# Attention on one core: the first query tile of each group without transposes on TensorE

## The chip, the cores and the metric

The kernel runs on one core of a Trainium2 chip. A core has a matrix engine (TensorE, PE in the profile, with its weight loads as PEld), a vector engine (VectorE, DVE), a scalar engine (ScalarE, ACT), a general one (GpSimd, POOL) and a queue that issues transfers (SyncE, SP). They run side by side and wait for each other by semaphores. PE's results land in PSUM, eight banks of 128 x 512 float32; DVE and ACT carry them from there to SBUF. The metric is the time on the device in microseconds, as the median of several runs.

## The reference

For x of 4 x 512 tokens with 256 features: a layer norm, then attention and a feed-forward gate on the normed tokens, and x + attention * gate at the end. There are 16 query heads of 128 and 4 key heads; query head h uses key head h mod 4, so a key head serves a group of four.

```python
xn = layernorm(x)
Q, K, V = xn @ Wq + bq, xn @ Wk + bk, xn @ Wv + bv     # 16, 4 and 4 heads of 128
scores = Q K^T / sqrt(128) + causal mask               # 512 x 512 of each head
ctx = softmax(scores) @ V
y = gelu(ctx @ Wo + bo)
s = layernorm(xn + y) * gamma + beta
g = silu((silu(xn @ Wgate) * (xn @ Wup)) @ Wdown)
out = x + s * g
```

All is float32, and the mask is causal: a query sees the keys up to its own place.

## The kernel before

A float32 product is made of three PE products. Each operand is split into `hi`, a rounded part, and `lo`, the rest; `product` (line 93) adds hi*hi, hi*lo and lo*hi into one PSUM bank (lines 95, 96 and 97). Splitting a bank is the work of `split_psum` (line 82): ACT writes `hi` (line 86, or 89 with a bias), then DVE writes `lo` (line 87, or 90).

The feed-forward gates of all four batches come first, up to about 150 us. The attention phase follows: 64 steps (b, g, i), for each batch b, group g and query tile i of 128 queries, i from 0 to 3 (in the very last group from 3 to 0). A query tile holds four sub-tiles of 32 queries (S = 32); one tile of scores has 128 rows, 32 queries of each of the four heads.

- `scores` (line 416) takes one sub-tile: PE makes the scores (for i = 0 with whole float32 operands, line 438), DVE adds the mask and takes the row's least (line 449), ACT takes exp and the row's sum (line 460), DVE inverts the sum (line 473), and POOL scales the row (line 474). The probabilities lie in `p`, rows of heads and queries, columns of keys. Two constant buffers of 128 x 4 x 512 serve in turn; a first query tile uses the last 128 of the 512 columns.
- `transposed_probs` (line 476) turns the 128 keys of block j so that keys are rows: four transposes on PE against the identity (line 481) into a bank "t", then a split into a pair of SBUF tiles `pT`, from a tag "pt" of four buffers.
- `weighted` (line 486) multiplies the turned probabilities with the values of block j: one `product` with 128 rows (keys), 128 weight columns (features) and 512 moving columns (four heads of 128 queries). The sum over j lies in the bank "c"; the last block's split adds the values' bias and gives `ctxT`.
- `projected` (line 505) multiplies `ctxT` with Wo, in steps of one head, into "y0" or "y1".
- `keys`, `values` and `queries` (lines 375, 386 and 401) make the operands of later steps; each puts its product in the bank "mm" once attention runs.

PSUM's eight banks are two "s" (scores), two "t", "mm", "c", "y0" and "y1".

The order around the change is written by hand. In the loop over the steps (line 632) each piece of work gets a position, a number from a table of constants, and the pieces are emitted in that order: scores of the next step, transposes and products of this one, the projection of the step before, and queries, keys or values for later ones. From the emitted order a scheduler, with its own costs, sets each engine's queue and gives buffers to tiles; within an engine's queue the order is then fixed, and a waiting instruction holds all that stand behind it. Transfers stand in SP's queue: transposed tokens and what the end of a batch wants (`reload`, `load_fin`), weights (`load_w`), and the output.

Of the kernel before, what the change touches and what calls it, by code (L numbers as in the profile page):

```python
# [17 lines left out]
P = 128  # L18
EPS = 1e-5
S = 32  # queries of a head in a tile of scores  # L20
# [6 lines left out]
def kernel(  # L27
    ctx: ExitStack,
    tc: tile.TileContext,
    x: bass.AP,  # [B, L, D]  # L30
    wq: bass.AP,  # [D, H*E]
    bqT: bass.AP,  # [E, H]
    wk: bass.AP,  # [D, KV*E]
    bkT: bass.AP,  # [E, KV]
    wv: bass.AP,  # [D, KV*E]
    bvT: bass.AP,  # [E, KV]
    wo: bass.AP,  # [H*E, D]
    bo: bass.AP,  # [D]
    gamma: bass.AP,  # [D]
    beta: bass.AP,  # [D]  # L40
    wguT: bass.AP,  # [D, 2*INTER]
    wdT: bass.AP,  # [INTER, D]
    out: bass.AP,  # [B, L, D]
):
    """Products of float32 operands run on the tensor engine as products of two
    parts each: hi, rounded to the engine's 12 significant bits, and lo, the exact
    rest. hi*hi + hi*lo + lo*hi, summed in float32, is the float32 product."""
# [6 lines left out]
    G = H // KV  # query heads of a key head: g, g + KV, ...  # L54
    INTER = wdT.shape[0]
    NT = L // P  # token tiles of a batch
    ND = D // P  # chunks of the model dimension
    NI = INTER // P  # chunks of the inner dimension
# [10 lines left out]
    @contextmanager  # L69
    def behind(*keys):  # L70
        """Queues what the block does behind these instructions on their engines."""
        with ExitStack() as stack:
            for k in keys:
                for ins in latest[k]:
                    stack.enter_context(tc.issue_after(ins.ins))
            yield

# [1 line left out]
    def pair(tag, bufs, name, n=512):  # L79
        return work.tile([P, 2, n], F32R, tag=tag, bufs=bufs, name=name)  # L80

    def split_psum(dst, src, bias=None):
        """dst[:, 0] = hi, dst[:, 1] = lo of a bank of PSUM (plus a bias per partition)."""
# [9 lines left out]
    def product(out_ap, lhs, rhs, first, last, **kw):  # L93
        """out += lhs^T rhs; lhs and rhs are (hi, lo)."""
# [4 lines left out]
    # The power -1/2 of a variance.  # L99
    mhalf = const.tile([P, NT], F32, name="mhalf")  # L100
    nc.gpsimd.memset(mhalf, -0.5)
    # Loads the scalar engine's table before it is needed.
# [11 lines left out]
    def load_w(name, views, hi_on=None, lo_on=None):  # L114
        """A slot of 1024 columns of weights, in two parts."""
# [17 lines left out]
    # Probabilities of a query tile: [32 queries of each head of a group, sub-tile of 32  # L133
    # queries, keys], the last key that the tile sees in the last column. What a sub-tile
    # doesn't see of the last P keys stays zero.
# [20 lines left out]
    # The first tokens and the first weights come in small pieces, in the order of their use.  # L156
# [14 lines left out]
    def split_first(f, lo_on=None):  # L171
        """The columns of f of the first slot of the gate's weights."""
# [8 lines left out]
    # Keeps the tensor engine busy until the first tokens are there, so that its clock is up by then.  # L181
# [22 lines left out]
    # What the attention phase wants back: the transposed tokens in two parts, and for  # L204
    # the end of a batch the normed tokens, gate * gamma and gate * beta + x.
# [13 lines left out]
    def transposed(b, t):  # L219
        """xT[b][c]: the normed tokens, transposed, of chunk c, in two parts."""  # L220
# [31 lines left out]

    # The last S keys that a tile of scores sees hold the diagonal of each head. Masked
    # before the scores are scaled.
# [41 lines left out]
    ff_tags = [("s", 2), ("s", 2), ("t", 2), ("t", 2), ("mm", 1), ("c", 1)]  # L296
    def h_tiles(b):
        """Places for the eight tiles of a batch among those of the attention phase."""
# [65 lines left out]
    banks = ["mm", "c"]  # "c" only until the first values are weighted  # L364
# [5 lines left out]
    def whole(dst, t):  # L370
        """The first P columns as they were before they were split: so few columns go
        faster through the tensor engine whole."""
        nc.gpsimd.tensor_tensor(dst, t[:, 0].bitcast(F32), t[:, 1].bitcast(F32), ALU.add)  # L373
# [12 lines left out]
    def values(b, t):  # L386
# [12 lines left out]
        vv[b, t] = v  # L399

    def queries(b, g, r):
# [6 lines left out]
        if r == 0:  # L408
            # [E, part, sub-tile of S queries, head of g, query]
# [6 lines left out]
    def scores(b, g, i, t):  # L416
        """Causal scores of sub-tile t of query tile i, of the four heads of g, as
        probabilities. Kept negated up to exp, so that the minimum of a row is the bias
        that exp wants."""
# [3 lines left out]
        if t == 0:  # L423
            if (b, g, i) in steps[-3:]:
                # Towards the end the slots of weights that are done with serve as well.
# [50 lines left out]
    def transposed_probs(b, g, i, j):  # L476
        p = probs[b, g, i][0]
        # From rows [head, query] of each sub-tile to columns [head, sub-tile, query].
# [7 lines left out]
    def weighted(b, g, i, j):  # L486
        """Transposed probabilities against the values: [E, heads of g, queries of i]."""
# [7 lines left out]
        if j == i:  # L495
            c = pair("stage" if (b, g, i) == steps[-1] else "ctx", 2, f"ctxT_{b}_{g}_{i}")
            # A row of probabilities sums to 1, so the values' bias comes in here.
# [36 lines left out]
    def finished(b, t, last):  # L534
        """Residual, second layer norm, gate and the outer residual of token tile t."""
# [213 lines left out]
```

## Time and profile before

| what | value |
|---|---|
| median of three runs | 681.08 us (680.22 to 681.22) |
| span of the profiled execution | 679.5 us |
| PE busy | 661.7 us, 97% of the span |
| PE weight loads busy | 581.6 us, 86% |
| DVE busy | 447.8 us, 66% |
| ACT busy | 402.6 us, 59% |
| POOL busy | 273.4 us, 40% |
| transposes of probabilities on PE (line 481) | 640, 273 ns each |
| products with the values on PE (lines 95 to 97, pc) | 480, 395 to 432 ns each |
| bytes moved by transfers | 34.7 MB |

One execution was profiled, and all durations come from it. Its span runs from the first to the last instruction; the runs' times are taken by themselves and are not sums of the profile's rows. In a row of the groups, the name before `<-` is written and the names after it are read: `pt` are turned probabilities in PSUM, `pT` their split in SBUF, `pc` the context's sum, `ctxT` its split, `ps` scores, `pq`, `pk` and `pv` queries, keys and values, `py` the projection. Durations of matmuls overlap, so how closely they follow one another is read from their starts. A row of stretches gives its bounds and length, then the busy time and number of instructions per engine, then the granted clock, the DMA share and GB/s. In the list of the steps' ends that the stretches follow, the mark is the end of the ACT half of a `ctxT` split.

### The profile page before, as it was taken

What the parts mean: (1) busy time and instruction counts of PE and PEld (TensorE: products, weight loads), DVE (VectorE), ACT (ScalarE), POOL (GpSimd) and SP (SyncE); (2) the same over time, 40 slices, a digit from 0 to 9 for tenths busy, and PEclk for the clock granted to TensorE, in tenths of its full rate; (3) what the DMA queues carried; (4) which work ended last, traced back from release to release, by engine and by line L of the source; (5) the groups of instructions that cost most, each with busy time, mean ns of one, the idle gap of its engine ahead of it and who ended that gap; (6) DMA issues with size and microseconds to landing.
All of it is one profiled execution on the core that took longest, in us unless ns stands there. A gap on an engine that the chain in (4) does not pass through costs nothing.

```text
span 679.5 us, 12006 instructions
## 1 busy us (share of the span) xinstructions
PE 661.7 (97%) x3996; PEld 581.6 (86%) x3996; DVE 447.8 (66%) x1337; ACT 402.6 (59%) x956; POOL 273.4 (40%) x490
## 2 busy tenths in 40 slices
PE   7979999999999999999999999999999999999995
PEld 6768888889889888888888898889888988888984
DVE  5864434165766766775787666668867766687867
ACT  4434333253765766677676665957666668576772
POOL 5588130720646423222353232216433323354332
PEclk8999999999999999999999999999999999999998
DMA  7753322211310100000022000002210000032000
GB/s 223 246 191 122 127 81 90 77 47 50 92 31 2 36 29 1 1 0 1 20 76 94 1 0 1 2 1 63 63 62 1 1 2 1 1 93 79 1 1 32
DMA packets 25262, 34.73 MB, mean 51 GB/s; under 512 B 2288, under 2 KB 18544, under 8 KB 25200
## 3 DMA queue, kind: packets, MB, share of 16 engines
q1 hardware_dynamic: 25200, 33.97, 15.4%
q8 instruction: 31, 0.51, 0.3%
q14 instruction: 31, 0.25, 0.1%
HBM read 21.38 MB, written 12.58 MB: 50 GB/s over the span
## 4 chain that ended last, share of the span: by engine, by line
PE 89%; DVE 4%; DMA 4%; issue 1%; ACT 1%; POOL 1%; SPq 0%; ACTq 0%; DVEq 0%; POOLq 0%
PE pt L481 10%; PE pc L96 5%; PE pc L95 5%; PE pc L97 5%; PE pq L95 5%; PE py L97 4%; PE ps L97 4%; PE ps L96 4%; PE pq L97 4%; PE pq L96 4%; PE py L95 4%; PE ps L95 4%; PE py L96 4%; PE pg L97 3%; PE pg L96 3%; PE pg L95 3%
## 5 line engine op out<-in xcount | busy, mean ns | idle before, releaser
L474 POOL TENSOR_SCALAR p<-p,total 128x320 f32<-128x320 f32 (+15 forms) x256 | 127.6, 505 | 195.5 <-DVE total L473 174.9
L460 ACT ACTIVATE p<-p,least 128x320 f32<-128x320 f32 (+15 forms) x256 | 133.2, 522 | 59.7 <-DVE least L449 51.0
L449 DVE CUSTOM_DVE_ANT_0 p<-ps,mask 128x320 f32<-128x320 f32 (+15 forms) x256 | 109.8, 435 | 42.6 <-PE ps L97 17.5
L86 ACT CAST pT<-pt 128x512 fp32r<-128x512 f32 x160 | 89.2, 587 | 60.0 <-PE pt L481 59.2
L87 DVE TENSOR_TENSOR pT<-pt,pT 128x512 fp32r<-128x512 f32 x160 | 106.6, 686 | 25.5 <-ACT pT L86 25.0
L481 PE MATMUL pt<-ident,p 128*128 128x128 f32 x640 | 107.2, 273 | 0.5 <-POOL p L474 0.5
L481 PEld LDWEIGHTS pt<-ident,p 128*128 128x128 f32 x640 | 81.1, 142 | 17.5 <-POOL p L474 0.7
L97 PE MATMUL py<-w_o,ctxT 128*128 128x256 f32 x256 | 73.5, 287 | 0.6 <-DVE ctxT L90 0.6
L95 PE MATMUL py<-w_o,ctxT 128*128 128x256 f32 x256 | 72.9, 285 | 0.1
L96 PE MATMUL py<-w_o,ctxT 128*128 128x256 f32 x256 | 72.1, 281 | 0.0
L96 PE MATMUL pc<-pT,v 128*128 128x512 f32 x160 | 69.1, 432 | 0.0
L95 PE MATMUL ps<-kT,qT 128*128 128x288 f32 (+3 forms) x192 | 68.5, 357 | 0.0
L373 POOL TENSOR_TENSOR q<-qT 128x128 f32<-128x128 f32 x64 | 30.4, 474 | 93.7 <-DVE qT L90 55.8
L95 PE MATMUL pc<-pT,v 128*128 128x512 f32 x160 | 64.5, 403 | 0.1
L97 PE MATMUL pc<-pT,v 128*128 128x512 f32 x160 | 63.2, 395 | 0.0
L473 DVE RECIPROCAL total<-total 128x1 f32<-128x1 f32 x256 | 38.4, 158 | 37.2 <-ACT p L460 35.1
L96 PE MATMUL ps<-kT,qT 128*128 128x288 f32 (+3 forms) x192 | 62.2, 324 | 0.0
L97 PE MATMUL ps<-kT,qT 128*128 128x288 f32 (+3 forms) x192 | 61.7, 322 | 0.0
L90 DVE SCALAR_TENSOR_TENSOR qT<-pq,bq_sb,qT 128x512 fp32r<-128x512 f32 x64 | 47.9, 748 | 15.3 <-ACT qT L89 15.3
L89 ACT ACTIVATE qT<-pq,bq_sb 128x512 fp32r<-128x512 f32 x64 | 44.0, 687 | 20.1 <-PE pq L97 19.6
L90 DVE SCALAR_TENSOR_TENSOR ctxT<-pc,bv_sb,ctxT 128x512 fp32r<-128x512 f32 x64 | 47.8, 747 | 11.1 <-ACT ctxT L89 10.5
L95 PE MATMUL pg<-xT,w_gu 128*128 128x512 f32 (+1 forms) x132 | 50.5, 397 | 3.9 <-DVE h L338 2.5
(127 smaller groups left out, 1567.5 us busy)
## 6 DMA issues: line engine op xcount, KB each, us to landing
fin<-fin_dram SPq DMA_DIRECT2D x16, 384.0 KB, 3.2
xT_dram<-xT SPq DMA_DIRECT2D x8, 512.0 KB, 2.6
fin_dram<-gate SPq DMA_DIRECT2D x16, 256.0 KB, 2.0
xT_again<-xT_dram SPq DMA_DIRECT2D x8, 512.0 KB, 3.9
fin_dram<-xn SPq DMA_DIRECT2D x16, 128.0 KB, 2.4
st_q<-in_wq_dram SPq DMA_DIRECT2D x8, 256.0 KB, 3.2
st_o<-in_wo_dram SPq DMA_DIRECT2D x4, 512.0 KB, 3.9
out_dram<-y SPq DMA_DIRECT2D x16, 128.0 KB, 1.7
```

The source lines that it names most:

```text
L86: first = nc.scalar.copy(hi, src)
L87: second = nc.vector.tensor_tensor(lo, src, hi.bitcast(F32), ALU.subtract)
L89: first = nc.scalar.activation(hi, src, AF.Identity, bias=bias)
L90: second = nc.vector.scalar_tensor_tensor(lo, src, bias, hi.bitcast(F32), ALU.add, ALU.subtract)
L95: nc.tensor.matmul(out_ap, lhs[0], rhs[0], start=first, stop=False, **kw)
L96: nc.tensor.matmul(out_ap, lhs[0], rhs[1], start=False, stop=False, **kw)
L97: nc.tensor.matmul(out_ap, lhs[1], rhs[0], start=False, stop=last, **kw)
L449: nc.vector.tensor_tensor_reduce(pr, ps[:, :seen], mask[:, L - seen :], scale=-SCALE, scalar=HIGHEST, op0=ALU.add, op1=ALU.min, accum_out= ...
L460: exp = nc.scalar.activation(pr, pr, AF.Exp, bias=least[:, r : r + 1], scale=-1.0, accum_out=total[:, r : r + 1],)
L473: latest["dve"] = [nc.vector.reciprocal(total[:, r : r + 1], total[:, r : r + 1])]
L474: latest["pool"] = [nc.gpsimd.tensor_scalar(pr, pr, total[:, r : r + 1], 1.0, ALU.mult, ALU.mult)]
L481: nc.tensor.transpose(pt[:, :, t], p[:, t, ts(j, P)], ident)
```

## The change

For a first query tile (i = 0) that is not among the last three steps, which is 15 of 16, the probabilities are no longer turned on PE. DVE transposes each sub-tile in blocks of 32 x 32: a block holds 32 queries of one head against 32 keys, so afterwards the rows are [head, 32 keys] and the columns [key block, sub-tile, query]. Blocks that the mask leaves empty are skipped. The result `u` lies in columns of the same constant buffer that this tile does not use, and ACT and DVE split it as before, now from SBUF.

The values have to meet these rows. `values` of the first token tile of a batch writes its pair to DRAM (`v_dram`), and `values_beside` reads it back for each group so that all four sets of 32 rows hold the same 128 keys as four blocks of 32 (`vr`, from the tag "pt"). `weighted` then makes, for each key block, each of the three parts and each head, a product of 32 rows whose place in the array is the head's row group. A key block c meets the queries from 32c on, so the columns are 128, 96, 64 or 32. Each head has its own PSUM bank, "c", "t", "t" and "mm", and is split by itself: four splits of 128 columns in place of one of 512.

`values_beside` is emitted for groups 1 to 3 at position 0.9 of the step with i = 2 of the group before, for group 0 of batches 1 to 3 at the start of the step that uses it, and for batch 0 ahead of the loop. Comments and docstrings are removed as well.

```diff
@@ values
         vv[b, t] = v
+        if t == 0:
+            nc.sync.dma_start(v_dram[b].rearrange("g p s e -> p s g e"), v.bitcast(F32).rearrange("p s (g e) -> p s g e", g=KV))
+
+    def values_beside(b, g):
+        vr[b, g] = work.tile([P, P // S, 2, E], F32R, tag="pt", bufs=4, name=f"vr_{b}_{g}")
+        for r in range(G):
+            nc.sync.dma_start(vr[b, g][ts(r, S)].bitcast(F32), v_dram[b][g].rearrange("(c k) s e -> k c s e", k=S))
+
+    vr = {}
+    v_dram = [dram.tile([KV, P, 2, E], F32, tag=f"v{b}", name=f"v_dram_{b}") for b in range(B)]
@@ transposed_probs
         p = probs[b, g, i][0]
+        if i == 0 and (b, g, i) not in steps[-3:]:
+            u = p_tiles[steps.index((b, g, i)) % 2][:, :, :P]
+            for t in range(NT):
+                nc.vector.transpose(
+                    u.rearrange("p c (t q) -> p c t q", q=S)[:, : t + 1, t],
+                    p[:, t, : (t + 1) * S].rearrange("p (c k) -> p c k", k=S),
+                )
+            t = pair("pt", 4, f"pT_{b}_{g}_{i}_{j}")
+            hi, lo = (t[:, k].rearrange("p (c n) -> p c n", c=NT) for k in range(2))
+            nc.scalar.copy(hi, u)
+            nc.vector.tensor_tensor(lo, u, hi.bitcast(F32), ALU.subtract)
+            pT[b, g, i, j] = t
+            return
@@ weighted
+        if i == 0 and (b, g, i) not in steps[-3:]:
+            tags = [("c", 1), ("t", 2), ("t", 2), ("mm", 1)]
+            pcs = [
+                psum.tile([P, P], F32, tag=tag, bufs=bufs, name=f"pc_{b}_{g}_{i}_{r}") for r, (tag, bufs) in enumerate(tags)
+            ]
+            t = pT.pop((b, g, i, j)).rearrange("p k (c n) -> p k c n", c=NT)
+            v = vr[b, g]
+            for c in range(NT):
+                at = ds(c * S, P - c * S)
+                for a, d in ((0, 0), (0, 1), (1, 0)):
+                    for r in range(G):
+                        nc.tensor.matmul(
+                            pcs[r][:, at],
+                            v[ts(r, S), c, a],
+                            t[ts(r, S), d, c, at],
+                            start=c == 0 and a == d,
+                            stop=c == NT - 1 and a == 1,
+                            skip_group_check=True,
+                            tile_position=(r * S, 0),
+                        )
+            c = pair("ctx", 2, f"ctxT_{b}_{g}_{i}")
+            for r in range(G):
+                latest["ctx"] = split_psum(c[:, :, ts(r, P)], pcs[r], bv_sb[:, g : g + 1])[:1]
+            ctxT[b, g, i] = c
+            return
@@ the loop over the steps
+    values_beside(0, 0)
     for s, (b, g, i) in enumerate(steps[:-2]):
         n = s % NT
         chunks = []
+        if n == 2 and b * KV + g + 1 < B * KV:
+            chunks.append((0.9, values_beside, divmod(b * KV + g + 1, KV)) if g + 1 < KV else (0.9, lambda: None, ()))
+        if n == 0 and g == 0 and b > 0:
+            values_beside(b, 0)
```

## The prediction

> **What bounds the kernel now.** I read the busy times and the chain that ended last first. The two lines below are from the profile's page: busy time, share of the span and instructions of each engine, then the chain's shares.
>
> ```profile
> PE 661.7 (97%) x3996; PEld 581.6 (86%) x3996; DVE 447.8 (66%) x1337; ACT 402.6 (59%) x956; POOL 273.4 (40%) x490
> ...
> PE 89%; DVE 4%; DMA 4%; issue 1%; ACT 1%; POOL 1%; SPq 0%; ACTq 0%; DVEq 0%; POOLq 0%
> ```
>
> TensorE (PE) carries 89% of the chain. But a busy PE need not be a full one, so the second view is one of stretches: each reaches from one ACT eviction of a context to the next and so holds one step that works on a first query tile (14 of them; the columns are length, then busy time and count per engine, then granted clock).
>
> ```profile
> core 0: us, PE busy (x) PEld busy (x) DVE busy (x) ACT busy (x) POOL busy (x), PEclk, DMA share, GB/s
> 269.82:274.09 4.27, 4.27 (x32) 3.98 (x30) 2.60 (x9) 3.09 (x8) 1.66 (x4) 1.00 0.00 0
> 331.82:339.55 7.73, 7.73 (x55) 7.05 (x54) 6.52 (x28) 5.69 (x18) 5.16 (x12) 1.00 0.15 33
> sum 74.52, PE 74.13 PEld 67.63 DVE 55.73 ACT 55.86 POOL 37.69; mean PE 5.29 PEld 4.83 DVE 3.98 ACT 3.99 POOL 2.69
> ```
>
> A mean stretch lasts 74.52 / 14 = 5.32 us; PE is busy for 5.29 of it, VectorE (DVE) for 3.98, ScalarE (ACT) for 3.99. So in the very steps that the change touches, a microsecond of PE is a microsecond of the kernel, while DVE has 1.34 us to spare and ACT 1.33. The clock is 1.00 there, so it explains nothing and offers nothing.
>
> What a product costs PE is not its duration (they overlap) but the distance between starts. The third view is the order of time on PE and on its weight loads (start, duration).
>
> ```profile
> 332.08 0.40 PE L95 MATMUL pq<-xT_again,w_q 128*128 128x512 f32 x1
> 332.31 0.39 PE L96 MATMUL pq<-xT_again,w_q 128*128 128x512 f32 x1
> 332.84 0.28 PE L96 MATMUL ps<-kT,qT 128*128 128x160 f32 x1
> 332.96 0.28 PE L97 MATMUL ps<-kT,qT 128*128 128x160 f32 x1
> 333.07 0.28 PE L481 MATMUL pt<-ident,p 128*128 128x128 f32 x1
> 334.10 0.19 PEld L97 LDWEIGHTS py<-w_o,ctxT 128*128 128x128 f32 x1
> 334.22 0.19 PEld L95 LDWEIGHTS py<-w_o,ctxT 128*128 128x128 f32 x1
> ...
> 396.06 0.60 PE L481 MATMUL pt<-ident,p 128*128 128x128 f32 x4
> ...
> 253.86 0.30 PE L438 MATMUL ps<-k,q 128*128 128x32 f32 x2
> ```
>
> 512 columns start 0.23 us apart (332.08, 332.31): the stream sets it. At 160 columns it is 0.11 to 0.12 (332.84, 332.96, 333.07), although 160/512 of 0.23 is 0.07; weight loads also start 0.12 apart (334.10, 334.22). So below some 256 columns a product costs its weight load, about 0.11 us, however narrow it is. Four transposes take 0.60 us with 0.27 for the last (its row's mean is 273 ns), so they start 0.33 / 3 = 0.11 apart. The shortest distance that the trace has is in the last line: two passes over 32 columns, 0.30 us together, where one lasts 0.275 at its longest: 0.03 us.
>
> **What the change removes.** It applies to 15 of the 16 first query tiles (that of the last group is among the last three steps). Off PE go four transposes, 4 x 0.11 = 0.44, and three products of 512 columns, 3 x 0.23 = 0.69: 1.13 us a step, 15 x 1.13 = 17 us in all. This is the most that can be won, 2.5% of the span.
>
> **What it puts on PE.** 4 key blocks x 3 parts x 4 heads = 48 products of 32 rows a step, each with a load of 128 weight columns, and 128, 96, 64 or 32 columns wide. The streams alone, four heads side by side, are 3 x 320 columns at 0.23/512 = 0.43 us. But all are in the narrow range, so what counts is the load, and the trace has no 32-row load. From below: 48 at the shortest distance, 48 x 0.03 = 1.3 us (12 quartets at one load each, 12 x 0.11, give 1.3 as well). From above: every load by itself, 48 x 0.11 = 5.3 us. Here two rules of the Trainium skill are weighed. "TensorE: Matmul & The Clock Gate", section LDWEIGHTS, says that a load of 32 rows takes as long as one of 128, since columns count: by it alone the 48 cost 5.3 us and the step loses 4.2. The same page, in its section on packing small matmuls, has different row groups overlap and gives 3.07 times the speed for four 32-row products: an estimate of 5.3 / 3.07 = 1.7 us. The trace can show neither; it only makes the load, not the stream, the thing to be shared. I take 1.55, between 1.3 and 1.7, since the order of the loop (heads innermost) puts each load on another row group than the one before.
>
> A second rule speaks against the change: "TensorEngine Tiling (Array Packing)", section Tiling Modes, says that a change of mode drains the engine. What a drain exposes I take from a transpose: 273 ns of duration less 110 of distance, 0.16 us, twice a step 0.33; without it the sum is 5 us lower. PE per step: 1.55 + 0.33 - 1.13 = +0.75.
>
> **What it puts on DVE and ACT.** Fixed cost and slope come from the score rows of two widths and from the context's rows.
>
> ```profile
> 397.13 0.39 DVE L449 CUSTOM_DVE_ANT_0 p<-ps,mask 128x224 f32<-128x224 f32 x1
> 397.57 0.48 ACT L460 ACTIVATE p<-p,least 128x224 f32<-128x224 f32 x1 [0.23 <-DVE least L449]
> 403.88 0.53 DVE L449 CUSTOM_DVE_ANT_0 p<-ps,mask 128x352 f32<-128x352 f32 x1
> 404.45 0.59 ACT L460 ACTIVATE p<-p,least 128x352 f32<-128x352 f32 x1
> ...
> L89 ACT ACTIVATE ctxT<-pc,bv_sb x64: 667/688/697, 176.5 to 669.1; 128x512 fp32r<-128x512 f32 x64
> L90 DVE SCALAR_TENSOR_TENSOR ctxT<-pc,bv_sb,ctxT x64: 721/750/755, 177.2 to 670.3; 128x512 fp32r<-128x512 f32 x64
> ```
>
> 128 more columns cost DVE 0.14 us and ACT 0.11. A context split of 128 columns is then 0.75 - 3 x 0.14 = 0.33 on DVE and 0.69 - 3 x 0.11 = 0.36 on ACT; four in place of one add 0.57 and 0.75. The four block transposes (32 to 128 columns, 320 together) have no row; with the fixed 0.19 of the context's row (0.75 - 4 x 0.14) and that slope they take 4 x 0.19 + 320/128 x 0.14 = 1.1 us. Half of that would be a fixed cost near zero, twice would be blocks moved at half speed. The split of the probabilities keeps its size (0.59 on ACT, 0.69 on DVE) and only reads SBUF. DVE goes to 3.98 + 0.57 + 1.1 = 5.65 a step, ACT to 4.74; PE to 6.04. So all of this stays behind PE, but DVE's cover shrinks from 1.34 to 0.4 us; if it were gone, the 1.7 us would be on the path, 15 x 1.7 = 25 us.
>
> **Banks.** The context's sums now take "c", both "t" and "mm" together. As heads are innermost, the four end together: from the last product to the last free bank it is 4 x 0.36 + 0.33 = 1.8 us (before: 0.69 + 0.75 = 1.4). Behind these waits on PE stand the next step's transposes (they want "t") and queries ("mm"), and the first product itself waits until the query before it has left "mm". What PE can do meanwhile is the projection of the step before (12 x 0.12 = 1.4) and scores (12 x 0.11 = 1.3), but these sit behind a DVE that is now nearly full. Bounds: 0 if the filler covers it, 1.8 if not. I take 0.4, nearer to 0, for the filler is larger than the wait.
>
> **Buffers and DMAs.** The values beside each other take one of the four "pt" buffers through the step before, where four transposed probabilities want four: the last must wait for the first product to be done with its own. PE waited on such splits in no row of its list of waits, so there is slack; I take 0.2 x 15 = 3 us (0 to 10). Four stores of 512 KB and 64 loads of 128 KB go on SP's queue; comparable ones land in 2.6 and 1.7 to 2.4 us. For groups 1 to 3 they start a step of some 10 us early: hidden. At the start of batches 1 to 3 the chain is values (the last split ends at 298.0 for batch 1), store 2.6, four issues, load about 2.4: ready near 303.5 if a buffer and the queue are free, and the context's products ended at 306.0. About 2 us of slack; SP's queue can also stand behind a transfer that waits for its own producer. I take 1 us x 3 = 3 (0 to 9).
>
> **Sum.** 15 x (0.75 + 0.4) = 17, + 3 + 3 = 23 us. The profiled execution's span is 679.5 us, so 702.5; the median of the runs is 681.08, 1.6 above the span, so 704.
>
> **Rivals.**
> - Half side by side: the loads overlap in pairs, 48 x 0.055 = 2.6 us. PE +1.8, bubbles 0.4: 15 x 2.2 + 6 = 39, 720 us. For it: nothing measured says that four loads share the way in.
> - Not side by side at all, so that the row groups don't do what they are said to: 5.3 + 0.33 - 1.13 = 4.5; the bubbles fall to 0.2 because PE gives DVE time. 15 x 4.7 + 6 = 76, 757 us. For it: the load's 0.11 us at every width, and the skill's rule on 32 rows. Against it: the packing rule.
> - DVE takes PE's place: block transposes at twice my price, 6.75 a step against PE's 6.04, in order behind scores that PE waits for: +0.7 x 15 on top, 715. Against it: the stretches of the second query tile, cut in the same way, have DVE busy for 5.05 of 7.47 us, so much of it is made up.
> - Faster: the quartet costs less than a load, because 32-row loads hide in each other and behind the streams. It decides at 1.13 / 12 = 0.094 us a quartet with no drain; with 0.43 of streams and 12 x 0.03, 0.8 us, it gives 15 x -0.33 = -5, 676. Against it: the 48 would have to start 0.016 us apart, half of the shortest distance in the trace.
>
> **How the numbers follow.** Four abreast 0.50 (704; its own range 691 to 718, from bubbles of 0 to 0.9 us and DMA terms of 0 to 9), in pairs 0.15, one by one 0.15, DVE as bound 0.07, faster 0.10, no change 0.03. A measurement of this kernel can tell about 0.2% from no change, 679.7 to 682.4. The range goes from 681, leaving out the faster case, to 757, leaving out half of the one-by-one case: less than 0.2 in all. Faster 0.10, same 0.03, slower 0.87.
>
> **What the profile after would show.** Right: the new products' starts lie about 0.03 us apart, 48 of them in 1.3 to 1.9 us; the first-tile stretches grow from 5.3 to some 6.5; DVE shows four transposes of about 0.2 to 0.35 us. Starts 0.11 apart are the one-by-one case. If PE idles before the new products or before "pt" and "pq" for more than 1 us a step, the bank term was too small; a PE wait for the values' DMA at three places is the DMA term. The prediction is wrong downward if the narrow products turn out not to pay for loads.

## The result and the profile after

The changed kernel takes 758.47 us (median of four runs, 752.47 to 759.83), the kernel before 681.15: a ratio of 1.1114, with a 95% interval from 1.1082 to 1.1145. That is 77 us more, where the prediction had 23 and its range ended at 757.

From the page of the changed kernel, the same two lines as of before:

```profile
PE 720.5 (95%) x4611; PEld 625.6 (83%) x4611; DVE 472.0 (62%) x1442; ACT 407.8 (54%) x1001; POOL 274.2 (36%) x490
...
PE 80%; DVE 8%; ACT 4%; DMA 4%; POOL 2%; issue 2%; SPq 1%; DVEq 0%; ACTq 0%; POOLq 0%
```

PE works 59 us longer, and yet its share of the chain falls from 89% to 80%: it does more and it waits more. DVE's share of the span falls from 66% to 62%, while its part of the chain grows from 4% to 8%: it ends more of the waits than before, but it did not become the bound. The granted clock, a mean of 0.994 before, is 0.963.

The stretches that hold a first query tile, cut in the same way (to the end of the last of the four splits):

```profile
314.58:328.71 14.13, 12.81 (x103) 11.39 (x102) 8.60 (x38) 8.41 (x27) 4.88 (x12) 0.99 0.26 75
543.32:549.59 6.27, 6.27 (x79) 5.60 (x79) 4.72 (x21) 4.79 (x17) 3.22 (x7) 1.00 0.01 1
577.51:583.26 5.75, 5.75 (x61) 5.36 (x61) 3.18 (x13) 3.17 (x12) 1.94 (x5) 0.80 0.01 3
sum 125.60, PE 121.59 PEld 107.79 DVE 87.15 ACT 84.11 POOL 57.28; mean PE 8.69 PEld 7.70 DVE 6.22 ACT 6.01 POOL 4.09
```

They grew from 5.32 to 8.97 us on the mean, and unevenly: 6.27 in group 2, 14.13 at the start of a batch. The third row has a clock of 0.80, which no such stretch of before had.

How the new products run is seen in the order of time on PE. First a step in which the schedule kept them together:

```profile
510.25 0.33 PE L527 MATMUL pc<-pT,vr 32*128 32x128 f32 x4
510.51 0.42 PE L95 MATMUL ps<-kT,qT 128*128 128x320 f32 x1
...
511.15 1.41 PE L527 MATMUL pc<-pT,vr 32*128 32x128 f32 x44
512.49 0.46 PE L95 MATMUL ps<-kT,qT 128*128 128x352 f32 x1
```

Forty-four products take 1.41 us with the last one's own 0.26 in it, so eleven quartets start 1.15 / 10 = 0.115 us apart: four row groups pay for one weight load. In the queries' rows the wait is plain. The page's groups of line 89 and line 373 (form, count, busy time and mean, then idle time ahead and what ended it), first before, then after:

```profile
L373 POOL TENSOR_TENSOR q<-qT 128x128 f32<-128x128 f32 x64 | 30.4, 474 | 93.7 <-DVE qT L90 55.8
...
L89 ACT ACTIVATE qT<-pq,bq_sb 128x512 fp32r<-128x512 f32 x64 | 44.0, 687 | 20.1 <-PE pq L97 19.6
```

```profile
L373 POOL TENSOR_TENSOR q<-qT 128x128 f32<-128x128 f32 x64 | 30.4, 475 | 142.0 <-DVE qT L90 119.3
L89 ACT ACTIVATE qT<-pq,bq_sb 128x512 fp32r<-128x512 f32 x64 | 43.9, 687 | 57.8 <-PE pq L97 57.3
```

ACT stands 57.3 us before the splits of queries because PE has not made them; before it was 19.6. POOL waits 119.3 us for their second half, before 55.8. Queries are late. They are made in the bank "mm".

**Where the 77 us went.** In the profiled execution of each kernel I summed the distances between neighbouring starts on PE from 165 us on. Each form has a distance of its own (0.108 us for a transpose; for other products 0.110, or the time of their columns if that is longer, 0.225 for 512). What exceeds it counts as half clock as far as the trace's clock records show half speed, as a wait if more than 0.15 us remains, and as small otherwise; the 32-row products are kept apart, with all the time to the next start. The sum for the attention phase is 507 us before and 584 after.

| us | before | after | difference |
|---|---|---|---|
| 32-row products | 0 | 36.4 | +36.4 |
| own distances of all others | 469.2 | 459.0 | -10.2 |
| small excess | 33.2 | 40.5 | +7.3 |
| waits | 4.8 | 30.6 | +25.8 |
| half clock on other products | 0.0 | 18.0 | +18.0 |

The 32-row products replace three products and four transposes a step (15 x (3 x 0.225 + 4 x 0.108) = 17 us; that time is gone from the second and third rows). So three things are to be explained: products, waits, clock.

### The profile page after: what moved, and what is told of

It is laid out like the page before. It is cut to its first block, busy times and chain, and to the rows that moved or that the text cites. A ratio compares the mean times of both kernels' runs of the same rounds, so it can differ in the third digit from the quotient of the medians.

```text
span 756.9 us, 13430 instructions
## 1 busy us (share of the span) xinstructions
PE 720.5 (95%) x4611; PEld 625.6 (83%) x4611; DVE 472.0 (62%) x1442; ACT 407.8 (54%) x1001; POOL 274.2 (36%) x490
## 3 DMA queue, kind: packets, MB, share of 16 engines
q1 hardware_dynamic: 38576, 44.46, 18.8%
## 4 chain that ended last, share of the span: by engine, by line
PE 80%; DVE 8%; ACT 4%; DMA 4%; POOL 2%; issue 2%; SPq 1%; DVEq 0%; ACTq 0%; POOLq 0%
PE pt L508 8%; PE py L95 4%; PE pc L527 4%; PE py L97 4%; PE pc L95 4%; PE pq L95 4%; PE ps L95 4%; PE pq L97 4%; PE pq L96 4%; PE py L96 4%; PE pc L96 4%; PE pc L97 4%; PE ps L97 3%; PE ps L96 3%; PE pg L97 3%; PE pg L96 3%
## 5 line engine op out<-in xcount | busy, mean ns | idle before, releaser
L461 DVE CUSTOM_DVE_ANT_0 p<-ps,mask 128x320 f32<-128x320 f32 (+15 forms) x256 | 109.8, 433 | 35.9 <-PE ps L97 17.7
L87 DVE TENSOR_TENSOR pT<-pt,pT 128x512 fp32r<-128x512 f32 x145 | 97.4, 685 | 29.0 <-ACT pT L86 28.4
L86 ACT CAST pT<-pt 128x512 fp32r<-128x512 f32 x145 | 81.4, 583 | 46.1 <-PE pt L508 44.2
L508 PE MATMUL pt<-ident,p 128*128 128x128 f32 x580 | 93.9, 283 | 0.0
L97 PE MATMUL py<-w_o,ctxT 128*128 128x256 f32 x256 | 79.3, 310 | 6.8 <-DVE ctxT L90 6.7
L508 PEld LDWEIGHTS pt<-ident,p 128*128 128x128 f32 x580 | 73.9, 146 | 11.8
L95 PE MATMUL py<-w_o,ctxT 128*128 128x256 f32 x256 | 78.6, 307 | 3.9 <-ACT ctxT L89 3.5
L373 POOL TENSOR_TENSOR q<-qT 128x128 f32<-128x128 f32 x64 | 30.4, 475 | 142.0 <-DVE qT L90 119.3
L89 ACT ACTIVATE qT<-pq,bq_sb 128x512 fp32r<-128x512 f32 x64 | 43.9, 687 | 57.8 <-PE pq L97 57.3
L96 PE MATMUL py<-w_o,ctxT 128*128 128x256 f32 x256 | 74.7, 292 | 0.0
L95 PE MATMUL ps<-kT,qT 128*128 128x288 f32 (+3 forms) x192 | 69.0, 359 | 4.5 <-DVE least L461 3.3
L90 DVE SCALAR_TENSOR_TENSOR ctxT<-pc,bv_sb,ctxT 128x128 fp32r<-128x128 f32 (+1 forms) x109 | 53.7, 524 | 21.7 <-ACT ctxT L89 21.6
L96 PE MATMUL ps<-kT,qT 128*128 128x288 f32 (+3 forms) x192 | 64.1, 334 | 0.0
L97 PE MATMUL ps<-kT,qT 128*128 128x288 f32 (+3 forms) x192 | 63.9, 334 | 0.0
L89 ACT ACTIVATE ctxT<-pc,bv_sb 128x128 fp32r<-128x128 f32 (+1 forms) x109 | 50.9, 510 | 20.8 <-PE pc L527 13.2
L96 PE MATMUL pc<-pT,v 128*128 128x512 f32 x145 | 61.4, 423 | 0.0
L95 PE MATMUL pc<-pT,v 128*128 128x512 f32 x145 | 60.6, 418 | 0.4 <-ACT pT L86 0.3
L95 PEld LDWEIGHTS py<-w_o,ctxT 128*128 128x128 f32 x256 | 51.3, 200 | 11.2 <-ACT ctxT L89 8.4
```

The costliest lines, as they stand in the source:

```text
L86: first = nc.scalar.copy(hi, src)
L87: second = nc.vector.tensor_tensor(lo, src, hi.bitcast(F32), ALU.subtract)
L89: first = nc.scalar.activation(hi, src, AF.Identity, bias=bias)
L90: second = nc.vector.scalar_tensor_tensor(lo, src, bias, hi.bitcast(F32), ALU.add, ALU.subtract)
L95: nc.tensor.matmul(out_ap, lhs[0], rhs[0], start=first, stop=False, **kw)
L96: nc.tensor.matmul(out_ap, lhs[0], rhs[1], start=False, stop=False, **kw)
```

## The experiments

Two theories stood at first. W: the four banks and their splits make PE wait, and the clock falls because PE waits. C: the clock falls because bursts of narrow products count as nearly idle. A third cause could be a transfer or a buffer. One table holds what all runs gave; "starts" counts the starts of 32-row products that come more than 0.015 us after the one before (all quartets together would be 180, or 60 with a third of the products; in the two kernels that keep head 3 apart 360 and 120), the other columns are those of the sum above. The time is the median of the runs, the rest is of the one execution that was profiled.

| kernel | time, us | clock | products | starts | waits | half clock |
|---|---|---|---|---|---|---|
| before | 681.15 | 0.994 | | | 4.8 | 0.0 |
| after | 758.47 | 0.963 | 36.4 | 307 | 30.6 | 18.0 |
| four_banks | 727.84 | 0.992 | | | 30.2 | 1.5 |
| third | 722.53 | 0.995 | 15.4 | 129 | 31.2 | 0.0 |
| heads_outer | 812.79 | 0.922 | 81.9 | 652 | 21.6 | 34.0 |
| vr_early | 756.74 | 0.971 | 34.7 | 252 | 35.8 | 15.2 |
| four_splits | 688.04 | 0.995 | | | 10.0 | 1.5 |
| mm_free | 691.31 | 0.992 | | | 4.4 | 0.0 |
| t_free | 720.18 | 0.994 | | | 27.8 | 0.0 |
| dve_beside | 684.75 | 0.990 | | | 7.5 | 1.5 |
| s_bank | 776.12 | 0.954 | 57.3 | 420 | 18.1 | 21.4 |
| mm_first | 775.69 | 0.953 | 48.6 | 358 | 34.1 | 23.7 |
| clock_up | 782.08 | 0.976 | 43.1 | 267 | 25.8 | 9.9 |
| vr_stage | 759.73 | 0.962 | 37.0 | 285 | 32.7 | 18.0 |
| mm_apart | 754.27 | 0.985 | 65.1 | 530 | 11.8 | 4.5 |
| mm_apart_third | 710.58 | 0.990 | 31.0 | 204 | 7.6 | 2.5 |

**Four banks on the kernel before**

```diff
@@ weighted, kernel before
+        if i == 0 and (b, g, i) not in steps[-3:]:
+            tags = [("c", 1), ("t", 2), ("t", 2), ("mm", 1)]
+            ...
+            for a, d in ((0, 0), (0, 1), (1, 0)):
+                for r in range(G):
+                    nc.tensor.matmul(pcs[r], v[:, a], t[:, d, ts(r, P)], start=a == d, stop=a == 1, skip_group_check=True)
+            c = pair("ctx", 2, f"ctxT_{b}_{g}_{i}")
+            for r in range(G):
+                latest["ctx"] = split_psum(c[:, :, ts(r, P)], pcs[r], bv_sb[:, g : g + 1])[:1]
```

> The kernel before, with one part of the change alone: the context of a first query tile is summed in four banks, one for each head (c, t, t, mm), by twelve full-array products of 128 columns in place of three of 512, and split in four. Transposes stay on PE, nothing is read back, the result is the same. Theory W (the four banks and their splits make PE wait, and the clock falls because PE waits): the gaps that the changed kernel shows, about 26 us, come back, with a granted clock below 0.98; 12 x 0.11 - 0.69 = 0.63 us of PE a step are 9.5 us more, so 715 to 730 us. Theory C (the clock falls because bursts of 32-row products count as a nearly idle engine): clock 0.99 or more, 9.5 us of PE and up to 6 us of waits, 690 to 697 us.

727.84 us, a ratio of 1.0676 (1.0645 to 1.0707), with a clock of 0.992. Neither theory had both right: the waits of W come back in full, 30.2 us, and without one narrow row group, but the clock does not follow them: it falls once in the attention phase short of the end, for one window, in which PE was busy for 1.95 of 3.41 us. So waits of this sum do not by themselves cost much clock. The waits show in one place where two queries follow each other (order of time on PE, ACT and DVE):

```profile
369.45 0.39 PE L97 MATMUL pq<-xT_again,w_q 128*128 128x512 f32 x1
369.88 0.69 ACT L89 ACTIVATE qT<-pq,bq_sb 128x512 fp32r<-128x512 f32 x1 [3.95 <-PE pq L97]
370.60 0.75 DVE L90 SCALAR_TENSOR_TENSOR qT<-pq,bq_sb,qT 128x512 fp32r<-128x512 f32 x1 [1.16 <-ACT qT L89]
371.40 0.50 PE L95 MATMUL pq<-xT_again,w_q 128*128 128x512 f32 x1 [0.56 <-DVE qT L90]
```

From the last product of one query to the first of the next, "mm" is held for 1.95 us by its split; PE fills 1.4 of it with other work and idles 0.56.

**A third of the products**

```diff
@@ weighted, changed kernel
-                for a, d in ((0, 0), (0, 1), (1, 0)):
+                for a, d in ((0, 0),):
 ...
-                            stop=c == NT - 1 and a == 1,
+                            stop=c == NT - 1,
```

> The changed kernel with only the hi*hi part of the 32-row products: 16 in place of 48 a step; hi*lo and lo*hi are left out, so the context of the first query tiles is rounded. All banks, splits, transposes and transfers stay. The bursts take 2.05 to 2.5 us at full clock; a third of them is about 0.8, so 1.2 to 1.7 us a step go, 18 to 25 us. Theory C: with the bursts short the clock stays at 0.985 or more, and another 12 to 18 us go: 715 to 728 us. Theory W: the waits and their half clock stay, 733 to 740 us with a clock of 0.96 to 0.97.

The context of the first tiles is then rounded, as hi*lo and lo*hi are left out. 722.53 us, clock 0.995, as theory C expected. Of the 35.9 us that go, 21.0 are products (36.4 to 15.4) and 18.0 half clock (to 0), 39 in all; the waits stay at 31.2. The same place in both kernels, ahead of, during and after a burst in group 3, as stretches; first the changed kernel:

```profile
577.60:581.00 3.40, 3.40 (x47) 3.10 (x47) 2.35 (x10) 1.94 (x8) 1.59 (x5) 1.00 0.02 5
581.00:587.80 6.80, 6.80 (x37) 6.67 (x37) 2.34 (x10) 3.01 (x9) 1.30 (x3) 0.50 0.00 0
587.80:591.20 3.40, 3.40 (x22) 3.12 (x21) 2.02 (x5) 1.20 (x3) 0.46 (x1) 1.00 0.00 0
```

and with a third of the products:

```profile
553.00:556.40 3.40, 3.40 (x29) 2.80 (x28) 3.40 (x15) 2.66 (x11) 1.26 (x3) 1.00 0.00 0
556.40:563.20 6.80, 6.80 (x47) 6.49 (x47) 4.27 (x17) 4.34 (x12) 2.92 (x6) 1.00 0.00 0
```

PE counts as busy through all of them. But in the changed kernel the burst is followed by 6.8 us at a clock of 0.50, with 37 products done in them; with the short burst the clock stays at 1.00, with 47.

**Heads outermost**

```diff
@@ weighted, changed kernel
-            for c in range(NT):
-                at = ds(c * S, P - c * S)
-                for a, d in ((0, 0), (0, 1), (1, 0)):
-                    for r in range(G):
+            for r in range(G):
+                for c in range(NT):
+                    at = ds(c * S, P - c * S)
+                    for a, d in ((0, 0), (0, 1), (1, 0)):
```

> The changed kernel with the loop over heads outermost: the same 48 products, but twelve of one row group one after another. If quartets of different row groups overlap now, this takes the overlap away: 48 loads at 0.11 us are 5.3 us a step in place of 2 to 2.5, 40 to 50 us more, 800 to 810 us, less what the earlier end of the first three banks gives back (up to 1 us a step, 785). If products of 32 rows cost the same in any order, 745 to 760 us.

812.79 us, 54 more than the changed kernel, a little beyond the expected 40 to 50. The order of time shows one such burst at full clock:

```profile
505.25 4.24 PE L527 MATMUL pc<-pT,vr 32*128 32x128 f32 x48 [0.39 <-DMA vr<-v_dram]
509.42 0.39 PE L95 MATMUL py<-w_o,ctxT 128*128 128x256 f32 x1
```

The 48 take 4.17 us to the next start, 0.087 each, where quartets took 1.6 in all. Over the kernel the products grow from 36.4 to 81.9 us and half clock from 18.0 to 34.0. Row groups side by side are real, and the overlap hangs on the order.

**Values loaded early, and in another buffer**

```diff
@@ vr_early: values_beside and the loop over the steps
-            ... .bitcast(F32), v_dram[b][g].rearrange(...)
+            ... .bitcast(F32), v_dram[b if g or b == 0 else b - 1][g].rearrange(...)
-            chunks.append((0.9, values_beside, ...) if g + 1 < KV else (0.9, lambda: None, ()))
-        if n == 0 and g == 0 and b > 0:
-            values_beside(b, 0)
+            chunks.append((0.9, values_beside, divmod(b * KV + g + 1, KV)))
@@ vr_stage: values_beside
-        vr[b, g] = work.tile(..., tag="pt", bufs=4, ...)
+        vr[b, g] = work.tile(..., tag="stage" if b else "pt", bufs=2 if b else 4, ...)
```

> The changed kernel, where the values of group 0 of batches 1 to 3 are loaded a step early like all others, from the copy of the batch before; so the context of 12 heads' first tiles is computed with another batch's values. It takes away the chain of store and load at the start of a batch. The steps of group 0 of batches 1 to 3 are 9 to 11 us longer than before, those of the other groups 2 to 6. If the chain is the cause of the difference, 3 x 6 = 18 us go: 738 to 742 us. If it is the bursts, the banks or the clock, 752 to 760 us.

> The changed kernel, where the values beside each other lie, in batches 1 to 3, in a buffer of the tag stage that is unused then, in place of one of the four pt buffers. So the transposed probabilities of 12 of the 15 steps before have four buffers again. My term for this was 0.2 us a step: 755 to 758 us. If the missing buffer is what makes PE wait, 1 us a step and more: below 746 us.

In vr_early, group 0 of batches 1 to 3 is weighed with the values of the batch before; vr_stage frees the buffer in batches 1 to 3 alone. 756.74 and 759.73 us: neither the chain of store and load nor the missing buffer costs anything that shows. Early loading did change the bursts at a batch's start (24 starts in place of 41 to 43), so the chain was there; the time went to the next wait. What makes group 0 long is seen when the same group, batch 1's first, is cut as a stretch from one fourth tile's context to the next, in four kernels. Before:

```profile
301.83:331.82 29.99, 29.93 (x177) 26.16 (x177) 19.42 (x54) 20.61 (x43) 7.55 (x15) 1.00 0.01 1
```

Changed:

```profile
314.58:355.44 40.86, 38.99 (x244) 33.95 (x243) 23.02 (x70) 25.11 (x57) 9.49 (x20) 0.96 0.13 39
```

four_banks, which loads nothing back:

```profile
302.40:343.42 41.02, 38.69 (x225) 32.26 (x223) 24.27 (x75) 26.42 (x62) 9.74 (x21) 1.00 0.00 1
```

mm_free, which follows:

```profile
304.49:335.08 30.59, 30.54 (x186) 26.89 (x186) 19.93 (x55) 21.18 (x45) 7.33 (x15) 1.00 0.00 1
```

The 11 us are in four_banks without a transfer, and gone as soon as "mm" is left alone. In the changed kernel part of the 11 is products and half clock (its 0.96), so the likeness of the two is partly chance.

**Which bank, or the splits**

```diff
@@ mm_free: four_banks with three banks
-            tags = [("c", 1), ("t", 2), ("t", 2), ("mm", 1)]
+            tags = [("c", 1), ("t", 2), ("t", 2)]
+            ...
+            pcs = [pcs[0][:, :P], pcs[1][:, :P], pcs[2][:, :P], pcs[0][:, P : 2 * P]]
@@ t_free: four_banks with two banks
+            tags = [("c", 1), ("mm", 1)]
+            ...
+            pcs = [pcs[0][:, :P], pcs[0][:, P : 2 * P], pcs[1][:, :P], pcs[1][:, P : 2 * P]]
@@ four_splits: weighted, kernel before
-            latest["ctx"] = split_psum(c, pc, bv_sb[:, g : g + 1])[:1]
+            parts = G if i == 0 and (b, g, i) not in steps[-3:] else 1
+            for r in range(parts):
+                at = ts(r, G * P // parts)
+                latest["ctx"] = split_psum(c[:, :, at], pc[:, at], bv_sb[:, g : g + 1])[:1]
```

> The kernel with four banks, but head 3 shares the bank c with head 0, so that mm stays with the queries and keys: three banks (c, t, t), same twelve products, same four splits. If the loss of the four banks (46 us, of which 9.5 are PE's narrower products) comes from mm: 690 to 700 us. If it comes from the two t: 720 to 728 us. If from the splits: 720 to 728 us as well, with four_splits slow too.

> The kernel with four banks, but two heads to a bank, c and mm: both t stay with the transposes. If the loss comes from the t banks: 690 to 700 us. If it comes from mm: 720 to 728 us. If from the splits: 720 to 728 us.

> The kernel before, with the splits alone: the context of a first query tile is summed in one bank by three products of 512 columns as before, and only its split is made in four pieces of 128 columns on ACT and DVE. Theory S (the 1.3 us that four splits add on the two engines make what stands behind them late): 705 to 715 us, most of what the kernel with four banks lost (46 us). Theory B (the banks are missing to others): 681 to 687 us.

691.31 us (1.0152, 1.01 to 1.0205), 720.18 (1.0576) and 688.04 (1.0104). Of the 46 us that four_banks lost, 727.84 - 691.31 = 36.5 are the bank "mm"; the rest is about what the twelve narrower products were expected to take (9.5). Leaving both "t" alone gives 7.7. Four splits in place of one cost about 6. These parts overlap (36.5, 9.5, 7.7 and 6 make 60, not 46), but "mm" is by far the largest. The waits of ACT on a query, in the list of who waited for whom, follow the time; four_banks first, then mm_free:

```profile
ACT qT L89 <- PE pq L97: 61.9, 37, 4.0
```

```profile
ACT qT L89 <- PE pq L97: 23.1, 37, 2.1
```

**Block transposes beside**

```diff
@@ transposed_probs, kernel before
+        if i == 0 and (b, g, i) not in steps[-3:]:
+            u = p_tiles[steps.index((b, g, i)) % 2][:, :, :P]
+            for t in range(NT):
+                nc.vector.transpose(
+                    u.rearrange("p c (t q) -> p c t q", q=S)[:, : t + 1, t],
+                    p[:, t, : (t + 1) * S].rearrange("p (c k) -> p c k", k=S),
+                )
```

> The kernel before with the block transposes on DVE beside its own: each first query tile is also turned in 32 x 32 blocks into the unused columns, and nothing reads it. Nothing else changes. My sum had them at 1.1 us a step, behind PE: 681 to 687 us, with a row of 0.2 to 0.35 us each. The rival in which DVE takes PE's place: 15 x 1.1 and more, 695 to 700 us.

684.75 us, a ratio of 1.0049 (1.0032 to 1.0066): 3 us, nearly all hidden. This is the load on DVE alone; as nothing reads the turned blocks, nothing here waits for them. In the changed kernel the transposes have these rows, with the splits of 128 columns (groups by form):

```profile
L90 DVE SCALAR_TENSOR_TENSOR ctxT<-pc,bv_sb,ctxT 128x128 fp32r<-128x128 f32 x60 | 17.3, 344 | 16.0 <-ACT ctxT L89 16.0
...
L495 DVE STREAM_TRANSPOSE p<-p 128x128 f32<-128x128 f32 x15 | 4.5, 299 | 0.7 <-POOL p L486 0.7
L495 DVE STREAM_TRANSPOSE p<-p 128x96 f32<-128x96 f32 x15 | 4.0, 269 | 0.4 <-POOL p L486 0.4
L495 DVE STREAM_TRANSPOSE p<-p 128x64 f32<-128x64 f32 x15 | 3.6, 238 | 1.2 <-POOL p L486 0.9
L495 DVE STREAM_TRANSPOSE p<-p 128x32 f32<-128x32 f32 x15 | 3.1, 206 | 3.0 <-POOL p L486 2.8
```

Together 1.01 us a step.

**Other banks in the changed kernel, and a fuller PE**

```diff
@@ s_bank
-            tags = [("c", 1), ("t", 2), ("t", 2), ("mm", 1)]
+            tags = [("c", 1), ("t", 2), ("t", 2), ("s", 2)]
@@ mm_first
+            tags = [("mm", 1), ("c", 1), ("t", 2), ("t", 2)]
@@ clock_up: ahead of each key block
+                k = kT[b, g][:, 0]
+                for m in range(2):
+                    f = 0 if c == 0 else P
+                    nc.tensor.matmul(pcs[0][:, f:], k[:, :P], k[:, f:], start=c == 0, stop=True, skip_group_check=True)
 ...
```

> The changed kernel, with one name altered: head 3 is summed in one of the two score banks s in place of mm. The four_banks kernel lost 46 us and only 10 once mm was left alone, so if mm is what costs in the changed kernel too, some 30 us go, less what the scores lose by having one bank for a while (0 to 15): 725 to 745 us. If the changed kernel's loss lies in its bursts and the clock alone, 750 to 765 us.

> The changed kernel, with the banks in another order: head 0 is summed in mm, so that mm is split first and comes free after 0.7 us in place of 1.8. If what costs is how long mm stays taken after the products, 15 x 1.1 = 16 us go: 740 to 745 us. If what costs is that the products must wait for mm to come free before they start, and hold it through the burst, 752 to 760 us.

> The changed kernel with more work on TensorE: ahead of each of the four key blocks of a first tile stand two full-array products of 512 or 384 columns into unread columns of the bank c, which nothing needs. They take 2 x 0.23 + 6 x 0.18 = 1.5 us a step and three more pairs of mode changes of about 0.3 us, 36 us in all at full clock. Theory C (the bursts count as a nearly idle engine): the granted clock goes to 0.985 or more and gives back the 18 to 22 us that half speed costs, so 768 to 778 us. If the clock has another cause: 0.96 as before and 790 to 800 us.

776.12, 775.69 and 782.08 us: three misses. In s_bank the waits do fall, from 30.6 to 18.1 us, but the scheduler, finding other banks free at other moments, takes the quartets apart: 420 starts in place of 307, 57.3 us of products in place of 36.4, and more half clock. It says little on "mm". In mm_first the waits stay (34.1) and the products are taken apart as well (358 starts, 48.6 us); its two runs lie 10 us apart. In clock_up half clock falls from 18.0 to 9.9 us and the mean clock rises to 0.976, but not to the 0.985 expected: the three bursts at the start of a batch, stretched to 6.8 to 8.5 us, still lower it, and so does one window without a 32-row product, in which PE was busy for 1.68 of 3.41 us. The time met neither forecast. More streaming kept the clock up wherever the burst was short; as a proof it is half of one.

**The changed kernel without mm**

```diff
@@ weighted, changed kernel
+            for heads in ((0, 1, 2), (3,)):
+                tags = {0: ("c", 1), 1: ("t", 2), 2: ("t", 2), 3: ("c", 1)}
+                ... the tiles, the loop over c and the parts (all three, or hi*hi alone), products of these heads
+                for r in heads:
+                    latest["ctx"] = split_psum(ctx_pair[:, :, ts(r, P)], pcs[r], bv_sb[:, g : g + 1])[:1]
```

> The changed kernel without the bank mm: heads 0 to 2 as now, side by side in c, t and t; head 3 follows alone in c, once head 0 has been split out of it. All 48 products and four splits stay. If mm is what makes the changed kernel wait (33 us of waits there, 33 in four_banks, none in mm_free), these go; the products grow from 12 quartets to 12 triples and 12 single ones, about 1.1 us a step or 17 us less what already runs apart (12 us), and longer bursts may lower the clock more: 730 to 745 us, with PE's gaps near those of before. If the waits in the changed kernel have another cause than in four_banks: 760 us or more.

> The same without mm, and with the hi*hi products alone (16 in place of 48, so the first tiles' context is rounded): both suspected causes are gone. If the loss is mm (36 us), the number of products with the clock that they lower (36 us) and little else, it comes to 684 to 695 us. If something else of the change costs (transposes on DVE, loads, buffers), over 700 us.

754.27 us: above the expected 730 to 745, and yet an answer on "mm". The waits fall from 30.6 to 11.8 us and half clock from 18.0 to 4.5; the products, apart by design (360 starts) and further by the order (530), grow from 36.4 to 65.1. They also lie spread over 10 us and more in nearly every step, with other work between them, so the clock's gain is not that of the waits alone. The sum of the three is -18.8 - 13.5 + 28.7 = -3.6, and -4.2 was measured. ACT's wait for queries falls with them:

```profile
ACT qT L89 <- PE pq L97: 31.0, 36, 2.1
```

So "mm" makes PE wait in the changed kernel as in four_banks, for 18.8 of its 30.6 us. With hi*hi alone it came to 710.58 us, above the expected 684 to 695. The kernel before took 682.44 beside it, so 28 us are left. Half of that is products: in ten of the fifteen steps the 16 start singly, 2.17 us in most of these, more than the 1.13 that was removed, and 31.0 - 17 = 14 in all. Waits (7.6 against 4.8) and half clock (2.5) make 5; about 9 us I cannot assign.

## Why the prediction was wrong

The direction was right, and so was most of the working on single rows. The time was not, and the number 757 of the one-by-one rival is near the result by chance: its mechanism is refuted, since heads_outer, where the loads do follow one by one, takes 54 us more.

- **What PE would save and the price of a quartet: right.** Four 32-row loads cost one: 0.112 to 0.115 us a quartet, against the 0.11 assumed. In nine steps the quartets stayed whole, and in the eight of these at full clock a burst of 48 takes 1.6 us with the ways back to the full array in it and 0.09 outside for each way in, where the prediction had 1.55 + 0.33. (Its lower bound of 48 x 0.03 is 1.4, not 1.3, which changes nothing.) The two rules of the Trainium skill, both in "TensorE: Matmul & The Clock Gate", hold together: a load of 32 rows does last as long as one of 128 (187 ns against 188, as its section LDWEIGHTS says), and the loads of different row groups share their time (its section on packing has a load overlap with a running product of another row group; its 3.07 is for 512 columns).
- **Products as a whole: too low.** 15 x 1.88 = 28 us were expected, 36.4 came. In six steps the scheduler took the quartets apart, at the start of a batch (41 to 43 starts, 3.5 to 4.2 us) and in group 3 (24 starts), and some ran at half clock. The prediction took the order of the loop for the order on the engine.
- **Banks: the step that failed most.** "I take 0.4, nearer to 0, for the filler is larger than the wait" stood with a bound of 1.8 us a step. In four_banks the bank "mm" alone costs 36.5 / 15 = 2.4. The bound counted the wait after the products, as if it came once. It left out the time ahead of them: all queries, keys and values pass through this one bank in a fixed order, each holding it for at least 2.8 us (1.4 of products, 1.4 of split), and what comes behind the new products is late in turn. The trace of the changed kernel shows both ends. From the first of the 48 products to the end of the split of "mm" it is 3.9 to 7.0 us, and in eight of the fifteen steps the bank stands empty for 3.8 to 8.0 us ahead of them, with its other users in line behind; in the kernel before and in mm_free it never stands empty for more than 3.2. That this makes up the 2.4 us is my reading; mm_first, which was to tell the two ends apart, ran its products in another order and does not decide it.
- **The clock: not in the sum at all.** "The clock is 1.00 there, so it explains nothing and offers nothing" read the profile of before as a promise for after. Half clock costs 18.0 us on other products, and more inside the bursts. Bursts bring on 31 of the 51 us that pass at half speed, idle windows of PE the rest (below).
- **DVE and ACT: right.** 1.01 us of transposes against 1.1, splits of 0.344 and 0.368 against 0.33 and 0.36. Their cover held in the test that was made: 3 us for the transposes alone. That DVE takes PE's place did not happen.
- **Buffers and DMAs: too high.** 3 + 3 us expected; vr_stage and vr_early show nothing.

The terms against what was measured: products less what they replace, 11 us expected, about 20 measured (36.4 less the 17 that went); banks 6, at most 33 (waits and small excess of the table, of which mm_apart shows 19 to be "mm"); clock 0, 18; DMA and buffers 6, about 0. These make 71 of the 77.

## What to carry to other kernels

A bank is priced by the whole queue that shares it: count how long each user holds it, before and after its work, and who is late next; here one small tile in the one bank that queries, keys and values share cost twice what the saved products were worth. Where a gain depends on instructions running side by side, look at the order on the engine, not in the source, and expect each change of banks or loads to change it. A PE that is "busy" with narrow work can lose its clock as one that waits does, so the columns streamed per few microseconds belong in the sum.

## What the runs showed of the hardware

**The clock goes with what is streamed, not with what is busy.** Half-speed stretches in the attention phase of the changed kernel last 3.4, 6.8 or 10.2 us, whole numbers of 3.41. I cut all sixteen traces, from 178 us to the last full window of products, into windows on that grid and counted the columns streamed in each, a 32-row product as a quarter of its columns. At the distance of 0.225 us for 512, a window holds 7,800 at most. Of the windows at full speed:

| columns streamed | PE busy for 90% or more: windows | followed by half speed | PE less busy: windows | followed by half speed |
|---|---|---|---|---|
| under 2,500 | 24 | 24 | 19 | 16 |
| 2,500 to 3,000 | 22 | 16 | 11 | 6 |
| 3,000 to 3,500 | 26 | 6 | 15 | 2 |
| over 3,500 | 2174 | 0 | 154 | 0 |

In the kernel before none of these windows held under 4,800. The two halves of the table agree: a busy PE keeps its clock no better than an idle one that streams as little. Both kinds occur in the changed kernel. Of its nine falls before the phase's end, five follow a window with a burst, with PE busy for 3.11 to 3.41 us of 3.41, and 31 us at half speed come of these. Four follow a window without a single 32-row product, with PE busy for 1.07 to 2.14 us, and 20 us come of these (the first of them lasts through the first burst). The longest single wait in them, 2.5 us for the split of a context, stands in PE's own list (us in total, times, longest), first before, then after:

```profile
PE py L97 <- DVE ctxT L90: 0.6, 2, 0.4
```

```profile
PE py L97 <- DVE ctxT L90: 6.7, 3, 2.5
```

The Trainium skill ("TensorE: Matmul & The Clock Gate", Part 1) has such windows, of 3413 ns, and a clock that falls to half after an idle one; the length agrees. Here a window that is busy, or one in which PE idles for 1.3 to 2.3 us of the 3.41, is enough. That the count of columns is the cause, and not something that goes with it, is supported by third (short bursts, waits as long in sum, no half speed) and partly by clock_up. The boundary is only as sharp as this count: with a lone 32-row product counted in full, windows of up to 4,700 columns are followed by half speed.

**A change between the two forms of the array is cheap.** After a full product of 352 columns the first 32-row product starts 0.252 us later, 0.093 more than the next full one would (0.159); after the last quartet a full product starts 0.187 us later, where the next quartet would take 0.112. That is about 0.17 us for both, half of what I had taken from a transpose's duration.

**A single row group without neighbours** starts a 32-row product every 0.087 us on the mean in the burst shown, less than the 0.11 of a full load. What sets this distance stays open.
